# Two graph layers on one core: left and right projections as one product by two levels of Strassen's recursion

## The chip, the cores and the metric

The kernel runs on one core of a Trainium2 chip, in fp32. The metric is the device time of one execution in microseconds, as the median of several runs; lower is better. The engines are named as the profile names them: PE (TensorE, with PEld for its weight loads), DVE (VectorE), ACT (ScalarE), POOL (GpSimd) and SP (SyncE, which only issues DMAs).

## The reference, cut to what matters

The input is 128 graphs of 64 nodes with 768 features, and one 64x64 adjacency for each graph. Layer 0 and layer 1 run one after the other, each with a residual and a layer normalisation:

```python
# layer 0, h = x
u = einsum('bld,bmd->blm', h, h) / sqrt(768); p = softmax(u)
attn = p * adjacency;  attn = attn / (sum(attn, axis=2) + 1e-10)
h_left, h_self, h_right = h @ W_left.T + b_left, h @ W_self.T + b_self, h @ W_right.T + b_right
ctx = attn[j > i] @ h_left + diag(attn) * h_self + attn[j < i] @ h_right
x = layernorm(x + relu(layernorm(ctx) * gamma + beta))
# layer 1: 12 heads of 64
q, k, v = x @ Wq + bq, x @ Wk + bk, x @ Wv + bv
scores = q k^T / 8 + beta * adj, masked where adj is 0
x = layernorm(x + softmax(scores) @ v)
```

Most of the arithmetic is in the six projections by 768x768 matrices: left, self and right in layer 0, q, k and v in layer 1.

## The kernel before

**Tiling.** The 8192 tokens are cut into 16 blocks of 512 tokens (four tiles of 128 tokens, eight graphs). A block needs for each projection a product of 512x768 by 768x768. Every such product is already done by one level of Strassen's algorithm in Winograd's form: tokens, inner dimension and columns are halved, and seven products of halves take the place of eight. `combined` forms the sums of the token side on POOL (S1, S2, S4 and one in place), `prepare` formed the sums of the weight side once at the start and left them in device memory (`pieces` for self, left, right and v; `qk_d` for q and k).

**The schedule of one projection** is the function `seven`. It walks through the seven factors in the order `ORDER` and for each through two halves j, and does three matmuls of 128x128 by 128x384 (q and k: by 128x256) into one PSUM bank. Two tags, X and Y, of two banks each hold the running sums. After each group of three, `first` or `last` evicts the bank: DVE adds the bias or an earlier part and writes SBUF (lines L301, L395, L413, L502); for q and k, ACT does part of it (L533, L539). The weights of a factor come from device memory by a load that SP issues (L296, L527) into the ring `wst` of four slots.

**The order of the work is written out by hand** (`manual_schedule`). In iteration n of the block loop stand, one after the other, the stages left, right and self of block n + 1, then v of block n, then q and k of block n for three groups of heads. In each stage, `hooks` put other work at given places: the scores and weighted sums of the block before (`scores`, `weighted`), the transposes of the adjacency product (`sides`), the context products (`context0`). Work of DVE and ACT in small pieces lies in two queues, `urgent` and `lazy`; after every group of matmuls `step` takes the next pieces off. `settle(key)` empties the queues of all pieces up to those of a key. `squares` and `turned` bring a block back transposed, through device memory (`x1d`), by loads of ACT's queue and transposes of DVE.

**What the change touches.** `side_part` does left or right, with `lr` as its target: four tiles of 128 x 2 x 768, in which the rows of one half of the partitions hold left, the others right, so that one matmul of `context0` (L428) can use both. `finish` is the last normalisation of a block: statistics on DVE (L242, L243), the normalisation on DVE (L629) and the stores of the output by POOL's queue (L630). The stores of a block's layer-0 result by POOL (L452) wait for DVE's L450.

Of the kernel before, what the change touches and what calls it, by code (L numbers as in the profile page):

```python
# [11 lines left out]
F32 = mybir.dt.float32  # L12
# [5 lines left out]
P = 128  # L18
# [5 lines left out]
T = 4  # L24
# [5 lines left out]
HP = H // 2  # L30
NHG = HC
# [11 lines left out]

@with_exitstack
def gnn_two_layers(ctx: ExitStack, tc, x, adj, wl, bl, ws, bs, wr, br, gamma, beta,
# [7 lines left out]
    tp = ctx.enter_context(tc.tile_pool(name="tp", bufs=2))  # L53
    l0 = ctx.enter_context(tc.tile_pool(name="l0", bufs=1))
    l0t = ctx.enter_context(tc.tile_pool(name="l0t", bufs=T))
    tmp = ctx.enter_context(tc.tile_pool(name="tmp", bufs=2))
    wst = ctx.enter_context(tc.tile_pool(name="wst", bufs=4))
# [20 lines left out]
    bias, affine_of = {}, {}  # L78
    bias["q"], bias["k"] = column(bq, "bq"), column(bk, "bk")
# [12 lines left out]
    for half in range(2):  # L92
        for g in range(2):
            sign = 1 if half == g else -1
            nc.gpsimd.affine_select(
                out=side[half * L : (half + 1) * L, g, :], in_=side[half * L : (half + 1) * L, g, :],
                compare_op=ALU.is_gt, fill=0.0, base=0, pattern=[[-sign, L]], channel_multiplier=sign,
            )


    blocks = {}

# [12 lines left out]

    GAP = (gap, "gap")

    def step(act_free=True):
        for queue in (urgent, lazy):
            if not queue:  # L120
                continue
            kind = queue[0][2] if len(queue[0]) > 2 else None
            if kind == "act" and not act_free:
                continue
            queue.popleft()[1]()
            if kind is None:
                return
# [14 lines left out]

    def prepare(nm, quarter_pool, sum_pool, waits=(0, 0, 0)):

        w = weights[nm].rearrange("(p c) e -> p c e", c=KC)
        src = {(0, 0): w[:, 0:HC, 0:HALF], (0, 1): w[:, 0:HC, HALF:D],
               (1, 0): w[:, HC:KC, 0:HALF], (1, 1): w[:, HC:KC, HALF:D]}
        b = {}  # L150
        for q in ((0, 0), (1, 0), (0, 1), (1, 1)):
            b[q] = quarter_pool.tile([P, HC, HALF], F32, tag="w", name=f"b{q[0]}{q[1]}_{nm}")

            with tc.issue_after(streamed["l"][2]) if nm == "k" else ExitStack():
                nc.sync.dma_start(out=b[q], in_=src[q])
        t5, t6, t4 = (sum_pool.tile([P, HC, HALF], F32, tag="w", name=f"t{i}_{nm}") for i in (5, 6, 4))
        in_sbuf = {1: b[0, 0], 2: b[1, 0], 3: b[1, 1], 5: t5, 6: t6, 7: b[0, 1], 4: t4}
        key = ("w", nm)
        if nm in "slrv":
            d = tc.dram_tile([4, P, HC, HALF], F32, name=f"d_{nm}")  # L160
            pieces[nm] = {1: src[0, 0], 2: src[1, 0], 3: src[1, 1], 5: d[0], 6: d[1], 7: d[2], 4: d[3]}

        def store(i):
            if nm in "slrv":
                if i in (5, 6, 7, 4):
                    nc.gpsimd.dma_start(out=pieces[nm][i], in_=in_sbuf[i])
            else:


                queue, first = (nc.sync, streamed["s"][6]) if nm == "q" else (nc.gpsimd, last_sum[1].ins)  # L170
                with tc.issue_after(first):
                    for hg in range(NHG):
                        queue.dma_start(out=qk_d[hg, i - 1, :, "qk".index(nm)],
                                        in_=in_sbuf[i][:, :, hg * P : (hg + 1) * P])

        def formed(i, out, left, right):
            nc.vector.tensor_tensor(out, left, right, ALU.subtract)  # L177
            store(i)

        def idle():  # L180
            pass

        later(key, *[idle] * waits[0], partial(formed, 5, t5, b[0, 1], b[0, 0]),
              *[idle] * waits[1], partial(formed, 6, t6, b[1, 1], t5), partial(formed, 7, b[0, 1], b[1, 1], b[0, 1]),
              *[idle] * waits[2], partial(formed, 4, t4, b[1, 0], t6))
        if nm in "qk":
            later(key, lambda: store(1), lambda: store(2), lambda: store(3))
        return in_sbuf
# [32 lines left out]
    def combined(xT, n=None):  # L221

        a11, a12 = xT[:, 0:HC, 0:HTOK], xT[:, HC:KC, 0:HTOK]
        a21, a22 = xT[:, 0:HC, HTOK:NTOK], xT[:, HC:KC, HTOK:NTOK]
        s1, s2, s4 = (tp.tile([P, HC, HTOK], F32, tag=f"S{i}", name=f"S{i}") for i in (1, 2, 4))
        nc.gpsimd.tensor_tensor(s1, a21, a22, ALU.add)
        nc.gpsimd.tensor_tensor(a21, a11, a21, ALU.subtract)
        nc.gpsimd.tensor_tensor(s2, s1, a11, ALU.subtract)
        last_sum[n] = nc.gpsimd.tensor_tensor(s4, a12, s2, ALU.subtract)
        return {1: a11, 2: a12, 3: s4, 4: a22, 5: s1, 6: s2, 7: a21}  # L230
# [23 lines left out]
    def seven(width, factors, first, last, hooks, taps_by_act=False):  # L254

        X, Y, u = {}, {}, {}  # L260
        for k, i in enumerate(ORDER):
            for j in range(2):
                for f in hooks.get(2 * k + j, ()):
                    f()
                if i == 1:
                    X[j] = ps_st.tile([P, 512], F32, tag="X", name="ps_X")
                if i in (2, 5):
                    Y[j] = ps_st.tile([P, 512], F32, tag="Y", name="ps_Y")
                ps = (X if i in (1, 6, 7, 4) else Y)[j][:, 0:width]
                fs = factors(i, j)  # L270
                for c, (a, b) in enumerate(fs):
                    nc.tensor.matmul(ps, lhsT=a, rhs=b, start=(c == 0 and i in (1, 2, 5)), stop=(c == len(fs) - 1),  # L272
                                     skip_group_check=True)
                if i == 1:
                    u[j, 1] = first(j, 0, ps)
                elif i == 2:
                    last(j, 0, 0, ps, u[j, 1])
                elif i == 6:
                    u[j, 2] = first(j, 1, ps)
                elif i == 7:  # L280
                    u[j, 3] = first(j, 1, ps)
                    last(j, 1, 1, Y[j][:, 0:width], u[j, 3])
                elif i == 4:
                    last(j, 1, 0, ps, None)
                elif i == 3:
                    last(j, 0, 1, ps, u[j, 2])
                step(not taps_by_act or (i, j) not in ((5, 1), (7, 0)))

    def by_tokens(nm, S, last, in_sbuf=None, hooks={}):
# [3 lines left out]
        def factors(i, j):  # L293
            if i not in wt:
                wt[i] = wst.tile([P, HC, HALF], F32, tag="w", name=f"w{nm}")
                streamed.setdefault(nm, []).append(nc.sync.dma_start(out=wt[i], in_=pieces[nm][i]).ins)  # L296
            return [(S[i][:, k, j * P : (j + 1) * P], wt[i][:, k, :]) for k in range(HC)]

        def first(j, b, ps):
            u = tmp.tile([P, HALF], F32, tag=f"u{b}", name="u", bufs=4 if b else 2)  # L300
            nc.vector.tensor_tensor(u, ps, bias[nm][:, b * HALF : (b + 1) * HALF], ALU.add)  # L301
            return u

        seven(HALF, factors, first, lambda j, m, n, ps, part: last(2 * m + j, n, ps, part), hooks)

# [11 lines left out]
    def attention0(n):  # L317
# [18 lines left out]
        blk["S"] = combined(xT, n)  # L336
# [63 lines left out]
    def side_part(n, nm, in_sbuf, hooks={}):  # L400
# [7 lines left out]
        def last(t, h, ps, part):  # L408
            cols = slice(h * HALF, (h + 1) * HALF)
            for g in range(2):  # L410
                rows = slice(g * L, (g + 1) * L)
                half = g if nm == "l" else 1 - g
# [3 lines left out]
        by_tokens(nm, blk["S"], last, in_sbuf, hooks)  # L416

# [99 lines left out]
    def projected(n, hg, hooks={}):  # L517
# [6 lines left out]
        def factors(i, j):  # L524
            if j == 0:
                wt[i] = wst.tile([P, 2, HC, P], F32, tag="w", name="wqk")
                nc.sync.dma_start(out=wt[i], in_=qk_d[hg, i - 1])  # L527
            return [(wt[i][:, j, k, :], S[i][:, k, :]) for k in range(HC)]

        def first(j, b, ps):  # L530
            u = tmp.tile([P, HTOK], F32, tag=f"u{b}", name="uqk", bufs=4 if b else 2)
# [14 lines left out]
    def scores(n, hg, at_once=1, pool=None):  # L546
# [8 lines left out]
        s = l1s_p.tile([P, T, 2, 2, L], F32, tag="s", name="s")  # L555
# [68 lines left out]

    def finish(n, tiles=range(T)):
# [28 lines left out]
    bias["l"] = row(bl, "bl")  # L654
# [3 lines left out]
    bias["r"] = row(br, "br")  # L658
# [28 lines left out]
    blocks[0]["S"] = combined(blocks[0]["xT"])  # L687
    start.close()
# [12 lines left out]
    for n in range(NBLK):  # L701
# [11 lines left out]

        last = n == NBLK - 1
        if p >= 0:
# [4 lines left out]
            at(three, 0 if not last else 6, finish, p)  # L720

        if not last:
            if n > 0:
# [32 lines left out]
                at(own, 11, sums1)  # L756
                if m + 1 < NBLK:
# [8 lines left out]
                side_part(m, "l", None, left)  # L766
                side_part(m, "r", None, right)
# [3 lines left out]
            if m + 1 < NBLK:  # L771
# [5 lines left out]

                def sums0():
                    settle(("t", m + 1))
                    attention0(m + 1)  # L780

                at(qk[0], 4, sums0)
# [3 lines left out]
        else:  # L786
            transposed1(n)
            at(qk[0], 9, lambda: later(("m", n), *mask(n), queue=urgent))
            blocks[n]["S"] = combined(blocks[n]["xT"])
        at(qk[1], 2, scores, n, 0)  # L790
# [45 lines left out]
```

## Time and profile before

| | |
|---|---|
| time, median of 3 runs (lowest, highest) | 2991.72 us (2988.51, 2993.49) |
| the profiled execution, own time | 2993.9 us |
| its span from the first to the last instruction | 2992.2 us |
| one block in the steady state, of that left, right, self, v, q and k | 182.26 us: 33.04, 27.09, 27.09, 33.64, 61.40 |
| busy share of PE, DVE, ACT, POOL | 98%, 72%, 23%, 11% |
| moved by DMA | 541.20 MB, mean 181 GB/s |

A line of the groups names the source line, the engine, the operation, what it writes and reads, its shape and count, then the busy time, the mean of one in ns, and the idle time of its engine before it with what ended it. One fp32 matmul stands as two records in the profile. In a line of the timeline the start and the length come first; instructions of one kind that follow each other are merged, with their count. "A <- B" says that A's wait ended with B.

### The profile page before, as it was taken

Reading aid. Unit: us, or ns where it says so; the run is one execution under the profiler, and the core shown is the slowest. Engines: PE = TensorE matmul, PEld = TensorE weight load, DVE = VectorE, ACT = ScalarE, POOL = GpSimd, SP = SyncE. Lnnn points to the kernel's source line nnn. Section 1 sums busy time; section 2 is a strip of 40 time slices with the busy share of each in tenths; the row PEclk is TensorE's granted clock in tenths of the full one; section 3 lists DMA queues with packets and bytes.
Section 4 is the critical chain, followed back from the end, with each engine's and each line's share of the span. In section 5 each row is a group of like instructions: output and inputs, shape, how many; then the busy total and the mean of one; then the engine's idle time right before and its main releaser. Section 6 shows DMA issues by size and latency. Waiting matters only on the chain.

```text
span 2992.2 us, 45095 instructions
## 1 busy us (share of the span) xinstructions
PE 2927.3 (98%) x17760; PEld 1981.9 (66%) x17760; DVE 2158.1 (72%) x4331; ACT 677.8 (23%) x1360; POOL 339.0 (11%) x297
## 2 busy tenths in 40 slices
PE   8999999999999999999999999999999999999996
PEld 5557667585675857658576675766758566585684
DVE  5857767677776777767777686777767777677657
ACT  0103214031140412304032140321404113040342
POOL 2131020110201101011110201102011020111010
PEclk9999999999999999999999999999999999999998
DMA  8673756747576574765847567475664757557343
GB/s 292 197 264 122 225 157 179 213 134 226 146 200 188 158 214 140 208 176 161 225 130 214 163 178 218 124 235 147 189 198 149 218 143 207 176 159 212 120 122 109
DMA packets 268130, 541.20 MB, mean 181 GB/s; under 512 B 28576, under 2 KB 173472, under 8 KB 267920
## 3 DMA queue, kind: packets, MB, share of 16 engines
q1 hardware_dynamic: 193824, 433.51, 47.3%
q10 hardware_dynamic: 60848, 44.05, 8.1%
q0 software_dynamic: 13248, 60.76, 5.0%
q8 instruction: 141, 2.31, 0.3%
q14 instruction: 69, 0.57, 0.1%
HBM read 473.37 MB, written 64.88 MB: 180 GB/s over the span
## 4 chain that ended last, share of the span: by engine, by line
PE 88%; issue 7%; DVE 3%; DMA 1%; POOL 1%; POOLq 0%; ACTq 0%; SPq 0%; DVEq 0%
PE ps_X L272 46%; PE ps_Y L272 35%; PE ps_ctx L428 3%; PE sc L563 2%; PE u L334 1%; PE ps_y L609 1%; DVE lr L413 1%; DVE eT L585 0%; DMA d_v<-t_v 0%; DMA b_s<-in_L_gnn_W_self_dram 0%; DMA b_k<-in_L_gnn_Wk_dram 0%; DVE o L438 0%; PE ps_a L382 0%; DVE t_s L177 0%; DMA bk<-in_L_gnn_bk_dram 0%
## 5 line engine op out<-in xcount | busy, mean ns | idle before, releaser
L272 PE MATMUL ps_X<-xT,wqk 128*128 128x256 f32 x1728 | 390.9, 380 | 3.4 <-ACT uqk L533 3.4
L533 ACT ACTIVATE uqk<-ps_X,bq 128x256 f32<-128x256 f32 x144 | 68.3, 474 | 1345.6 <-PE ps_X L272 1345.2
L272 PEld LDWEIGHTS ps_X<-xT,wqk 128*128 128x128 f32 x1728 | 329.7, 191 | 52.1 <-ACT uqk L533 3.8
L581 ACT ACTIVATE eT<-s 32x256 f32<-32x256 f32 x768 | 317.7, 414 | 149.8 <-DVE s L590 139.7
L272 PE MATMUL ps_Y<-S,wqk 128*128 128x256 f32 x1152 | 264.3, 379 | 0.0
L413 DVE TENSOR_TENSOR lr<-ps_Y,u 64x384 f32<-64x384 f32 x384 | 213.0, 555 | 66.3 <-PE ps_Y L272 57.1
L272 PEld LDWEIGHTS ps_Y<-S,wqk 128*128 128x128 f32 x1152 | 218.9, 190 | 29.8
L272 PE MATMUL ps_X<-wv,xT 128*128 128x384 f32 x576 | 195.3, 489 | 0.1
L242 DVE BATCH_NORM_STATS2 stats<-o 128x6 f32<-128x384 f32 x384 | 190.2, 537 | 0.4
L272 PE MATMUL ps_X<-wl,hT 128*128 128x384 f32 x540 | 185.4, 489 | 1.5 <-DVE u L301 1.5
L272 PE MATMUL ps_X<-ws,hT 128*128 128x384 f32 x540 | 182.4, 493 | 3.0 <-DVE u L301 3.0
L272 PE MATMUL ps_X<-wr,hT 128*128 128x384 f32 x540 | 179.1, 486 | 0.0
L619 DVE SCALAR_TENSOR_TENSOR o<-ps_y,rz,o 128x64 f32<-128x64 f32 x768 | 165.0, 278 | 6.8
L272 PEld LDWEIGHTS ps_X<-wv,xT 128*128 128x128 f32 x576 | 108.1, 190 | 81.3 <-issue 9.0
L272 PEld LDWEIGHTS ps_X<-ws,hT 128*128 128x128 f32 x540 | 103.7, 193 | 76.6 <-DVE u L301 3.6
L272 PEld LDWEIGHTS ps_X<-wr,hT 128*128 128x128 f32 x540 | 102.5, 190 | 71.3
L301 DVE TENSOR_TENSOR u<-ps_X,bv 128x384 f32<-128x384 f32 x96 | 52.9, 551 | 129.3 <-PE ps_X L272 129.3
L272 PEld LDWEIGHTS ps_X<-wl,hT 128*128 128x128 f32 x540 | 100.3, 190 | 64.0 <-DVE u L301 2.2
L541 DVE TENSOR_TENSOR q<-ps_Y,uqk 128x256 f32<-128x256 f32 x144 | 60.1, 418 | 112.4 <-ACT uqk L533 59.8
L272 PE MATMUL ps_X<-S,wqk 128*128 128x256 f32 x576 | 138.2, 385 | 0.0
L272 PE MATMUL ps_Y<-xT,wqk 128*128 128x256 f32 x576 | 135.6, 385 | 0.0
L272 PE MATMUL ps_Y<-wv,S 128*128 128x384 f32 x384 | 133.2, 490 | 0.0
(183 smaller groups left out, 4489.1 us busy)
## 6 DMA issues: line engine op xcount, KB each, us to landing
wqk<-qk_d SPq DMA_DIRECT2D x336, 384.0 KB, 3.0
wv<-d_v SPq DMA_DIRECT2D x64, 576.0 KB, 4.7
ws<-d_s SPq DMA_DIRECT2D x60, 576.0 KB, 4.5
wl<-d_l SPq DMA_DIRECT2D x60, 576.0 KB, 4.7
wr<-d_r SPq DMA_DIRECT2D x60, 576.0 KB, 4.7
wv<-in_L_gnn_Wv_dram SPq DMA_DIRECT2D x48, 576.0 KB, 4.0
ws<-in_L_gnn_W_self_dram SPq DMA_DIRECT2D x45, 576.0 KB, 3.9
wl<-in_L_gnn_W_left_dram SPq DMA_DIRECT2D x45, 576.0 KB, 4.3
```

The source lines that it names most:

```text
L242: nc.vector.bn_stats(stats[:, h, :], tiles[t][:, h * HALF : (h + 1) * HALF])
L272: nc.tensor.matmul(ps, lhsT=a, rhs=b, start=(c == 0 and i in (1, 2, 5)), stop=(c == len(fs) - 1), skip_group_check=True)
L301: nc.vector.tensor_tensor(u, ps, bias[nm][:, b * HALF : (b + 1) * HALF], ALU.add)
L334: nc.tensor.matmul(u[g * L : (g + 1) * L, t, :], lhsT=xT[:, c, tok], rhs=xT[:, c, tok], start=(c == 0), stop=(c == KC - 1))
L413: nc.vector.tensor_tensor(lr[t][half * L : (half + 1) * L, g, cols], ps[rows], bias[nm][rows, cols] if part is None else part[rows], ALU.add)
L428: nc.tensor.matmul(ps[g * L : (g + 1) * L, 0:HALF], lhsT=blk["aT"][:, t, g * L : (g + 1) * L], rhs=blk["lr"][t][:, g, cols], start=True, s ...
L533: nc.scalar.activation(u, ps, AF.Identity, bias=bias["qk"[j]][:, c : c + 1])
L541: nc.vector.tensor_tensor(dst, ps, part, ALU.add)
L563: nc.tensor.matmul(sc[r][g * L : (g + 1) * L, t, c, :], lhsT=q[rows, c, tok], rhs=k[rows, c, tok], start=True, stop=True)
L581: nc.scalar.activation(e[cols, :, rows], pairs[rows, :, cols], AF.Exp)
L609: nc.tensor.matmul(y[r, h][cols, t, c, :], lhsT=eT[rows, 2 * h + t, c, cols], rhs=v[rows, 2 * h + t, g, hg + c * HC, :], start=True, stop= ...
L619: nc.vector.scalar_tensor_tensor(res[:, r, c, hg, :], ps[:, t, c, 0:HD], rz[:, t, c : c + 1], res[:, r, c, hg, :], ALU.mult, ALU.add)
```

## The change

**Left and right as one product.** From block `DEEP` = 3 on, `both_sides` takes the place of the two calls of `side_part`. Its columns are the left and right columns side by side (2 x 192 in one matmul). On the first level there are seven factors as before; each is done by a second level of the same recursion (`nested`): tokens 256 into 2 x 128, columns 384 into 2 x 192, and of the three inner chunks of 128 two by the recursion and the third in the ordinary way. A second-level product is one matmul (j = 1, 6, 7) or two (j = 2, 5, 4, 3), and is evicted by one instruction into `u_deep` or straight into a quarter of the result. The first-level sums of the results are formed in place in `lr`, partly on POOL. The token side's second-level sums come from `second_level` on POOL. The products of two factors overlap: the order is 6, 5, 7 of one, 1, 2 of the next, 4, 3 of the first.

**Weights.** `deepened` makes the second-level weight sums from `pieces` in iterations 0 and 1 and leaves them in `lr_d`: nine matrices for each of seven factors. All weights of the block loop now come in chunks of 128x384 (192 KB) into a ring of 19 slots, where whole factors of 384 to 576 KB came into four.

**The rest.** Left always lies in the lower partitions of `lr`, right in the upper; for blocks from 3 on, ACT copies swap two of the four parts (`swapped`, in the self stage), and `side` changes with it. `finish_by_act` does the last normalisation with ACT (two passes with sums, one that normalises), except for the block before the last and the last. `step` has a `light` form that runs no DVE piece except tiny ones. S1, S2 and S4 are single buffers, the fourth sum has a function of its own (`combined4`), and the sums of the next block are formed in the third head group and not in the first.

```diff
+ORDER2 = (7, 1, 2, 6, 5, 4, 3)
+MATRICES = (1, 2, 8, 3, 9, 5, 7, 4, 6)
+DEEP = 3
...
-    wst = ctx.enter_context(tc.tile_pool(name="wst", bufs=4))
+    wst = ctx.enter_context(tc.tile_pool(name="wst", bufs=19))
...
-    def step(act_free=True):
+    def step(act_free=True, light=False):
...
+            if light and (queue is lazy or kind is None):
+                return
...
+    def deepened(i):
...
+        def begin():
+            for j, nm in enumerate("lr"):
+                src = pieces[nm][i]
+                for k in range(2):
+                    w[j, k] = wst.tile([P, 2, QUAD], F32, tag="w", name="w_deep")
+                    nc.sync.dma_start(out=w[j, k], in_=src[:, k, :].rearrange("p (h c) -> p h c", h=2))
...
+        def formed(j):
+            b11, b12, b21, b22 = (w[j, k][:, h, :] for k in range(2) for h in range(2))
+            for out, a, b in ((b11, b12, b11), (b12, b22, b12), (b22, b22, b11), (b21, b21, b22)):
+                nc.vector.tensor_tensor(out, a, b, ALU.subtract)
...
+    def second_level(F):
...
+        h0, h1 = slice(0, P), slice(P, 2 * P)
+        q = s2_p.tile([P, 5, P], F32, tag="q", name="q")
+        nc.gpsimd.tensor_tensor(q[:, 0, :], F[:, 0, h1], F[:, 1, h1], ALU.add)
+        nc.gpsimd.tensor_tensor(q[:, 1, :], q[:, 0, :], F[:, 0, h0], ALU.subtract)
+        nc.gpsimd.tensor_tensor(q[:, 3:5, :], F[:, 0::2, h0], F[:, 0::2, h1], ALU.subtract)
+        nc.gpsimd.tensor_tensor(q[:, 2, :], F[:, 1, h0], q[:, 1, :], ALU.subtract)
...
+                wt[i] = [wst.tile([P, HALF], F32, tag="w", name=f"w{nm}") for _ in range(HC)]
+                for k in range(HC):
+                    load = nc.sync.dma_start(out=wt[i][k], in_=pieces[nm][i][:, k, :])
...
+    def nested(width, sums, load, multiply, view, C, bias0, bias1, hooks):
...
+        def taken(i, q, ps, dst, add):
+            if add is None:
+                nc.scalar.copy(dst, view(ps))
+            else:
+                nc.vector.tensor_tensor(dst, view(ps), add, ALU.add)
...
+        def sub(i, j):
...
+            if j == 1:
+                X[i] = ps_st.tile([P, 512], F32, tag="X", name="ps_X")
+            if j in (2, 5):
+                Y[i] = ps_st.tile([P, 512], F32, tag="Y", name="ps_Y")
+            ps = (X if j in (1, 6, 7, 4) else Y)[i][:, 0:width]
+            multiply(F[i], W[i], j, ps)
...
+            step(len(done) > 8, j in (5, 1, 4))
...
+            for j in (6, 5, 7):
+                sub(i, j)
+            if after:
+                sub(after, 1)
+                sub(after, 2)
+            for j in (4, 3):
+                sub(i, j)
...
+    def both_sides(n, hooks):
...
+        def load(i):
+            w = {}
+            for k in (1, 2, 8, 6, 5, 9, 7, 4, 3):
+                w[k] = wst.tile([P, HALF], F32, tag="w", name="wlr")
+                nc.sync.dma_start(out=w[k], in_=lr_d[i - 1, MATRICES.index(k)].rearrange("p s c -> p (s c)"))
+            return w
...
+        def swapped(t):
+            low, high = lr[t][0:L, 1, :], lr[t][L:P, 0, :]
+            swap = l1s_p.tile([P, T * 4 * L], F32, tag="s", name="swap")
+            nc.scalar.copy(swap[0:L, 0:D], high)
+            nc.scalar.copy(high, low)
+            nc.scalar.copy(low, swap[0:L, 0:D])
...
-            at(three, 0 if not last else 6, finish, p)
+            at(three, 0 if not last else 6, finish if last else finish_by_act, p)
...
+                if m < DEEP:
+                    side_part(m, "l", None, left)
+                    side_part(m, "r", None, right)
...
+                else:
+                    for t, f in enumerate(both_sides(m, {**left, **{2 * len(ORDER) + k: f for k, f in right.items()}})):
+                        at(own, 1 + t, f)
```

## The prediction, made before the changed kernel was run

> **What bounds the kernel now.** I read the page's busy times and chain first, then a table of busy time by stage for one block in the middle, then the timeline of single banks.
>
> ```profile
> PE 2927.3 (98%) x17760; PEld 1981.9 (66%) x17760; DVE 2158.1 (72%) x4331; ACT 677.8 (23%) x1360; POOL 339.0 (11%) x297
> ...
> PE 88%; issue 7%; DVE 3%; DMA 1%; POOL 1%; POOLq 0%; ACTq 0%; SPq 0%; DVEq 0%
> ```
>
> TensorE (PE) is the bound, 98% busy and 88% of the chain. The stages of one block (left, right, self, values, queries and keys) say it more sharply; the columns are length, then busy us of PE, weight loads, VectorE (DVE), ScalarE (ACT), GpSimd (POOL), clock, DMA share, GB/s:
>
> ```profile
> 1585.17:1618.21 33.04, 31.70 (x282) 19.33 (x281) 24.38 (x53) 12.39 (x28) 1.63 (x3) 1.00 0.84 222
> 1618.21:1645.30 27.09, 27.09 (x86) 15.96 (x85) 22.86 (x59) 0.20 (x1) 1.08 (x2) 1.00 0.70 220
> 1645.30:1672.39 27.09, 27.09 (x86) 15.96 (x85) 19.25 (x27) 0.00 (x0) 8.10 (x6) 1.00 0.74 217
> ```
>
> Right and self take the same 27.09 us although DVE, POOL and DMA differ: there PE waits for nobody. A stage holds 42 products of 128x384, two records each (84), so one record is 27.09/84 = 0.3225 us, and the chain has the same: 24 records in 7.74 us.
>
> ```profile
> 1633.85 7.74 PE ps_X L272 x24
> ```
>
> Left has 5.94 us more: score and weighted products of the block before, and transposes, hooked in between. So fewer records pay in full, as long as PE still waits for nobody. Two timeline excerpts say how long a wait for a bank (PSUM) would be.
>
> ```profile
> 1585.17 2.10 PE L272 MATMUL ps_X<-wl,hT 128*128 128x384 f32 x6
> ...
> 1587.31 0.56 DVE L301 TENSOR_TENSOR u<-ps_X,bl 128x384 f32<-128x384 f32 x1 [0.92 <-PE ps_X L272]
> ```
>
> The sixth record's slot ends at 1585.17 + 6 x 0.3225 = 1587.105; DVE starts 0.20 us later and takes 0.56 (0.555 in the groups of L413).
>
> ```profile
> 128.14 0.54 DVE L301 TENSOR_TENSOR u<-ps_X,bs 128x384 f32<-128x384 f32 x1
> ...
> 128.75 3.52 PEld L272 LDWEIGHTS ps_X<-ws,S 128*128 128x128 f32 x12 [0.55 <-issue]
> 128.78 4.11 PE L272 MATMUL ps_X<-ws,S 128*128 128x384 f32 x12
> ...
> 132.73 4.03 PE L272 MATMUL ps_Y<-ws,S 128*128 128x384 f32 x12
> ```
>
> Here PE had waited for an eviction: released 0.07 us after its end (128.68), and twelve records later it stands at 132.73, not 128.78 + 3.87 = 132.65: a restart costs about 0.1 us more, the weight load that is no longer hidden. From the end of a product to the restart of a product that needs its bank: 0.20 + 0.555 + 0.06 + 0.10 = **0.915 us**, with DVE free.
>
> ```profile
> 1599.71 0.55 DVE L301 TENSOR_TENSOR u<-ps_X,bl 128x384 f32<-128x384 f32 x1
> 1600.17 0.17 DVE L615 RECIPROCAL rz<-ps_y 128x4 f32<-128x4 f32 x1
> 1600.38 0.86 DVE L619 SCALAR_TENSOR_TENSOR o<-ps_y,rz,o 128x64 f32<-128x64 f32 x4
> 1601.15 0.17 DVE L615 RECIPROCAL rz<-ps_y 128x4 f32<-128x4 f32 x1
> ```
>
> Back to back, DVE starts the next instruction 0.46 us after an eviction (I use 0.49), and one queued piece of "added" work lasts 1601.15 - 1600.17 = 0.98 us.
>
> **What the Trainium skill says.** "VectorE: DVE Perf Modes", its section on the TRN2 errata, prices a PSUM read at 120 + 384 cycles of 0.96 GHz = 525 ns; the trace has 555, which I use. "SBUF — State Buffer", Who interferes with whom: an instruction of DVE with one SBUF input doesn't contend with GpSimd, one with two does. The trace agrees: beside a POOL sum an eviction keeps 0.56 us, while the SBUF-only sum of L485 takes 1.92 us for 256 elements. The new POOL work therefore doesn't lengthen evictions. "DMA: Bandwidth & Descriptors", Specifications, gives 435 GB/s as the fabric's ceiling; this trace moves 386 GB/s from 9 to 30 us, at a share of 1.06, and I take that as full.
>
> **The change part by part.** *Fewer products.* From block 3 on, left and right become 7 x 7 sub-products of 128x(2x192), 11 matmuls for each of 7 instead of 12: 77 for 84. Saved: 7 matmuls = 14 records = 4.515 us a block, 13 blocks: **-58.7 us**, all on the path.
>
> *New waits for banks.* Before, between two uses of a bank lay the other half's three matmuls, 1.935 us, against 0.915 needed. Now a product with j = 1, 6, 7 is one matmul (0.645 us), the others two (1.29); the order for one factor i is 6, 5, 7, 1', 2', 4, 3 (' = next factor), 7.095 us. Each tag has two banks, and 2 and 5 each open a Y bank: 5 of the next factor takes the bank of 3, and only 6 lies between. Wait A: 0.915 - 0.645 = 0.27 us, six times a block, 1.62. Wait B: in the last factor 4 follows 7 directly, 0.92. Wait C: the queued pieces. The two "weighted" hooks each put four pieces of 0.98 us behind evictions. Where one follows 3's eviction (0.20 to 0.69), 6's eviction runs from 1.67 to 2.22 and 7 can start at 2.38, where it was due at 0.915 + 1.29 = 2.205: 0.18, about twice a block, 0.36. In all 2.90 us a block, x 13 = **+37.7 us**. Bounds: 1.5 us a block if the restart is hidden and C vanishes; 5.8 if evictions of the new form take 0.70 instead of 0.555. DVE's demand in a factor with four pieces is 7 x 0.49 + 4 x 0.98 = 7.35 us for 7.4: just enough.
>
> *DVE and ACT.* Evictions of left and right: 44 before (12 of L301, 32 of L413), 49 now, 4 of them ACT copies: DVE's sum is unchanged. The normalisation that ends a block leaves DVE (8 x 0.537 + 4 x 0.208 + 4 x 0.68 = 7.9 us) for 12 ACT passes of 768. ACT's rows of 256 (0.475) and 1536 (1.475 us) make 0.875 for 768: 10.5 us, and 12 swap copies of 64x768 as much, where ACT has 41.6 of 182 us now. It relieves a DVE that delays nobody: counted at nothing. DVE's tiny steps wait for the sums (3.5 us) 4.5 us after they could start. If ACT is late, the evictions behind those steps are, then PE; a us or two a block is the upper bound. The swaps stand in the self stage, 27 us, before the context that needs them.
>
> *POOL.* Per block 28 instructions of second-level sums (640 elements a factor) and 12 sums of 384. At L226's 1.81/768 = 2.4 ns an element, an estimate, that is 10.6 + 10.9 us in a stage where POOL is busy 2.7 us. A factor's sums can start when 3 of the factor before last ends and are first needed by its 6, 7 us later. Behind the x1d issues, which wait for DVE's normalisation (L450), stand the sums of the third factor, due well after. First-level sums move to the last head group, since their buffers are single: 7.7 us of products cover two of 1.81. Counted at nothing; if late, each us is on PE.
>
> *DMA and SP.* Left and right load 63 x 192 KB = 12.4 MB instead of 8.3; with what else moved (222 and 220 GB/s over 60.1 us, 13.3 MB) 17.4 MB in some 58 us, 300 GB/s of 386. Nineteen slots let a load start 8 to 9 us before its use; landing took 4.7 us for 576 KB. All weights of a block are 147 issues on SP for 49, at 0.33 us (the tile view of d_v): 48 of 180 us. The stores of the output and x1d stay on POOL. Hidden; at worst 2 or 3 us a block, where the transposing loads of sq (207 GB/s at a share of 1.10) coincide.
>
> *Start.* Making the deep weights: 56 subtractions of 192 elements on DVE (about 0.35 us each, by L301's size), 28 loads and 56 POOL issues, beside the products of blocks 0 to 2. I take +3 us; -4 to +8, since chunks can also arrive earlier.
>
> Sum: -58.7 + 37.7 + 3 = -18.0. The profiled execution took 2993.9 us (span 2992.2), 2.2 above the median 2991.7: 2975.9 there, **2974** as a median.
>
> **Rivals.** *All saved* (0.10): the waits are hidden, -58.7 + 3, 2936. For it: PE never waits in the stages shown. Against: only one matmul lies between the uses of the Y bank. *DVE as the bound* (0.15, the slower side): the form 2x192 or its SBUF operand costs more than 0.555. At 0.70, spaced 0.66, A is 0.41, B 1.06, and factors with four pieces need 8.5 us of DVE for 7.1: 5.8 us of waits a block, +16 us, with the start +19, 3011. It decides from about 0.64 us an eviction, where the waits reach 4.5. Against it: 64x384 and 128x384 forms both take 0.555. *Weights late* (0.10): 2.5 us more a block, +32.5 on my sum, 3006; for it, DMA shares of 0.84 already, and packets of 1.5 KB. *No gain* (0.08): the recursion saves 14 records but the start and small waits by ACT and POOL eat the rest, 2990.
>
> **How the numbers follow.** My case has 0.57, with 2962 to 2988 as its own range. About 0.2% (6 us) is what a measurement of this kernel tells from no change. My case's upper end adds to "same", its rest and the first rival to "faster": 0.68 faster, 0.15 same, 0.17 slower. The range leaves out most of the first rival and the worst of two others: 2950 to 3002.
>
> **What would show it.** In the profile after, left and right together should take 60.1 - 1.6 = 58.5 us; PE should show idle of 0.2 to 0.3 us behind DVE's L416 at each fifth product, 0.9 at the end; evictions of L416 0.55; POOL some 22 us more a block; s, v and q/k stages unchanged at 27.09, 33.64, 61.40. I'm wrong if that stage is under 56 or over 60 us, if L416 takes over 0.64, or if PE waits there for DMA or POOL.

## The result, and the profile after

The changed kernel takes **2977.3 us** (median of 5 runs, 2975.3 to 2979.7) where the kernel before took 2991.7 beside it (5 runs, 2988.5 to 2993.7): 0.9954 times as long, 95% interval 0.9939 to 0.9968. That is 14.4 us less, where 18 had been forecast. The profiled execution has a span of 2978.0 us (before 2992.2).

The page's busy times and chain, changed kernel:

```profile
PE 2881.8 (97%) x17578; PEld 1940.8 (65%) x17578; DVE 2062.7 (69%) x4219; ACT 994.4 (33%) x1848; POOL 713.0 (24%) x881
...
PE 79%; DVE 6%; issue 6%; ACT 5%; DMA 3%; POOL 1%; SPq 0%; ACTq 0%; POOLq 0%; DVEq 0%
```

PE works 45.5 us less but is busy for a smaller share, and the chain, 88% PE before, now passes through DVE and ACT for 11%: part of the saving has turned into waits. The table by stage (same columns as before) says where. The first row is left and right of a middle block, now one stage, the second is self:

```profile
685.87:743.87 58.00, 55.31 (x352) 32.33 (x350) 42.65 (x102) 26.17 (x53) 30.41 (x46) 1.00 0.97 291
743.87:770.96 27.09, 27.09 (x86) 15.96 (x84) 17.88 (x24) 9.96 (x12) 5.56 (x3) 1.00 0.81 238
```

Left and right were 33.04 + 27.09 = 60.13 us and are 58.00: 2.1 us a block, of the 4.515 that seven matmuls fewer make. Self, values and q/k kept 27.09, 33.64 and 61.40 to 0.01 us. So the sum of the profiled execution is: 13 blocks x -2.12 = -27.6; the start, up to the first such stage, +14.15 (505.75 us from the span's start instead of 491.60); a few late weights in three blocks +4.6, which the runs below hardly showed again; and from the last such stage to the end -5.2. Together -14.1, against spans 14.2 apart. Of the -5.2, 4.1 lie between the issue of the last store and the end of the span, 8.03 us before and 3.94 after. The packets of that store take 2.3 us in both; what differs is the time from the last packet to the end, 5.8 us and 1.7. The profile doesn't say why, so this part is no work that the change saved. The start also varies: in the runs below that leave its preparations as they are, the first such stage begins between 504.6 and 511.3 us. The two big terms are what the experiments are about.

**Inside a steady stage.** I took the distance of each matmul record from the last and noted what it has above 0.3225 us. Four waits and the hooks make up the 2.39 us that were paid back: product 6 of the first factor (number 7) 1.66; product 7 of two factors, for the bank of 6, 0.45 each; the last product 4 0.92; the score hook 0.42 more than before, the second weighted hook 1.52 less, since it no longer waits for transposes. The timeline around the first of these:

```profile
687.12 3.39 ACT L796 ACTIVATE eT<-s 32x256 f32<-32x256 f32 x8
...
690.31 0.46 POOL L314 TENSOR_TENSOR q<-hT 128x128 f32<-128x128 f32 x1
690.53 0.48 ACT L414 COPY u_deep<-ps_X 128x384 f32<-128x384 f32 x1
690.54 1.30 DVE L800 STREAM_TRANSPOSE eT<-eT 128x512 f32<-128x512 f32 x2 [2.85 <-ACT eT L796]
...
691.11 0.88 PE L613 MATMUL ps_X<-wlr,q 128*128 128x384 f32 x2 [1.43 <-POOL q L314]
```

The bracket blames POOL, as does the list of PE's waits (1.4 us here, 17.0 in all). But two instructions end just ahead of the restart: POOL's sum at 690.77 and ACT's copy at 691.01, which is the eviction of the bank that this product needs. 691.11 is 0.10 after the copy, close to the 0.07 that the prediction read between an eviction's end and the restart. And the copy is late because eight exponentials stand before it in ACT's queue. They were no later before the change. There the stage began at 1585.17, and this line stands in its timeline:

```profile
1586.41 3.40 ACT L581 ACTIVATE eT<-s 32x256 f32<-32x256 f32 x8
```

The exponentials end 4.64 us after the stage's start, as they do now (690.51 against 685.87), but no eviction of left or right was ACT's. Two suspects, then; the first experiment parts them.

The eviction itself behaves as forecast:

```profile
L416 DVE TENSOR_TENSOR lr<-ps_Y,u_deep 128x384 f32<-128x384 f32 x273 | 151.5, 555 | 75.1 <-PE ps_Y L613 66.9
```

**At the start.** The left stage of the second pass (for block 2) takes 48.75 us instead of 33.03:

```profile
334.79 2.50 DVE L666 TENSOR_SCALAR o<-o,mv,rstd 128x768 f32<-128x768 f32 x4
335.76 2.35 POOL L668 DMA_DIRECT2D x1d<-o  x4 [22.17 <-DVE o L666]
...
342.04 2.92 ACTq L275 DMA_DIRECT2D sq<-x1d  x3
...
346.29 3.40 ACT L796 ACTIVATE eT<-s 32x256 f32<-32x256 f32 x8
...
349.72 1.30 DVE L800 STREAM_TRANSPOSE eT<-eT 128x512 f32<-128x512 f32 x2 [6.83 <-ACT eT L796]
...
350.58 2.01 PE L824 MATMUL ps_y<-v,eT 64*64 64x65 f32 x64 [13.76 <-DVE eT L800]
```

Read from below: PE waits 13.8 us for transposed exponentials, DVE for ACT, and ACT issues its second half only after it has got the reloads `sq<-x1d` off, whose source was stored late, since all four pieces of the normalisation (L666) came from 334.8 on. Ahead of them DVE runs subtractions of `deepened`, 4.62 us from 303.3 and 1.54 us from 333.1. In the kernel before, the four pieces (L450) began at 305.4, 308.6, 309.9 and 323.3, and all the exponentials went out ahead of the reloads:

```profile
322.81 6.81 ACT L581 ACTIVATE eT<-s 32x256 f32<-32x256 f32 x16 [8.84 <-DVE s L590]
323.29 0.67 DVE L450 TENSOR_SCALAR o<-o,mv,rstd 128x768 f32<-128x768 f32 x1
...
329.34 2.41 ACTq L205 DMA_DIRECT2D sq<-x1d  x4
```

### The profile page after: what moved, and what is told of

It reads as the page before. It is cut to its first block, busy times and chain, and to the rows that moved or that the text cites. A ratio compares the mean times of both kernels' runs of the same rounds, so it can differ in the third digit from the quotient of the medians.

```text
span 2978.0 us, 49826 instructions
## 1 busy us (share of the span) xinstructions
PE 2881.8 (97%) x17578; PEld 1940.8 (65%) x17578; DVE 2062.7 (69%) x4219; ACT 994.4 (33%) x1848; POOL 713.0 (24%) x881
## 4 chain that ended last, share of the span: by engine, by line
PE 79%; DVE 6%; issue 6%; ACT 5%; DMA 3%; POOL 1%; SPq 0%; ACTq 0%; POOLq 0%; DVEq 0%
PE ps_X L362 32%; PE ps_Y L362 24%; PE ps_Y L613 9%; PE ps_X L613 8%; PE ps_ctx L644 3%; ACT eT L796 3%; PE u L504 1%; PE ps_y L824 1%; PE sc L778 1%; DMA wlr<-lr_d 1%; ACT L796 1%; DVE lr L416 1%; DVE mx L804 1%; DVE s L782 1%; DVE s L805 0%
## 5 line engine op out<-in xcount | busy, mean ns | idle before, releaser
L296 POOL TENSOR_TENSOR S<-hT 128x768 f32<-128x768 f32 x16 | 28.9, 1808 | 1157.3 <-PE ps_Y L362 1120.3
L613 PE MATMUL ps_Y<-wlr,q 128*128 128x384 f32 x546 | 208.6, 491 | 0.0
L416 DVE TENSOR_TENSOR lr<-ps_Y,u_deep 128x384 f32<-128x384 f32 x273 | 151.5, 555 | 75.1 <-PE ps_Y L613 66.9
L613 PE MATMUL ps_X<-wlr,q 128*128 128x384 f32 x364 | 150.1, 494 | 23.9 <-POOL q L314 17.0
L416 DVE TENSOR_TENSOR u_deep<-ps_X,lr 128x384 f32<-128x384 f32 x195 | 107.8, 553 | 60.4 <-PE ps_X L613 54.7
L613 PEld LDWEIGHTS ps_Y<-wlr,q 128*128 128x128 f32 x546 | 101.6, 190 | 67.2
L296 POOL TENSOR_TENSOR S<-xT 128x768 f32<-128x768 f32 x16 | 28.9, 1806 | 452.3 <-DVE xT L284 323.8
```

What stands on the lines that cost most here:

```text
L416: nc.vector.tensor_tensor(dst, view(ps), add, ALU.add)
L613: nc.tensor.matmul(ps, lhsT=a, rhs=b, start=(k == 0 and j in (1, 2, 5)), stop=(k == len(fs) - 1), skip_group_check=True)
```

## The experiments

In this part "the stage" is that of left and right of a steady block, and a ratio is to runs of the kernel before on the same chip.

**Who holds product 6 of the first factor?**

```diff
-            taken(i, q, ps, U[i, k], part(i, q))
+            if (i, k) == (7, 1):
+                nc.vector.tensor_copy(U[i, k], view(ps))
+            else:
+                taken(i, q, ps, U[i, k], part(i, q))
```

> One edit to the changed kernel: the very first eviction of a left-and-right stage (factor 7, product 1) is a DVE copy and no longer an ACT copy. Theory: product 6 of factor 7 waits 1.66 us a block for this eviction, because ACT still runs eight exponentials of the stage before (3.4 us) when the product is ready; on DVE it is done in time, 13 x 1.66 = 21.6 us go, 2955 to 2958 us. Rival: the wait is for the second-level sums of POOL, as the list of waits names it (L314); then nothing changes, 2975 to 2980 us.

Measured: 2971.65 us, ratio 0.9928 (0.9913 to 0.9943); the stage 57.30, 0.69 less and not 1.66. Its timeline:

```profile
691.87 0.81 PE L616 MATMUL ps_X<-wlr,q 128*128 128x384 f32 x2
...
692.65 0.45 POOL L314 TENSOR_TENSOR q<-hT 128x128 f32<-128x128 f32 x1
...
692.88 1.30 DVE L803 STREAM_TRANSPOSE eT<-eT 128x512 f32<-128x512 f32 x2 [2.39 <-ACT eT L799]
...
695.29 0.54 DVE L416 TENSOR_TENSOR lr<-ps_Y,u_deep 128x384 f32<-128x384 f32 x1
...
695.88 1.56 PE L616 MATMUL ps_Y<-wlr,hT 128*128 128x384 f32 x4 [0.62 <-DVE lr L416]
```

Product 6 now runs at 691.87, without a wait and before POOL's sum has begun: POOL was never the cause. But DVE stands 2.39 us for the same exponentials, to transpose them, and the next evictions stand behind it: PE stops 0.89 us in another place, and one of the 0.45 grows by 0.08. 1.66 - 0.97 = 0.69. The cause isn't which engine copies; it is that the exponentials end 4.6 us after the stage begins.

**Is the predicted wait A absent because of how banks are handed out?** The prediction had product 5 wait for the bank of the factor's own predecessor, 0.27 six times. Here each Y bank gets its own fixed use:

```diff
-                Y[i] = ps_st.tile([P, 512], F32, tag="Y", name="ps_Y")
+                Y[i] = ps_st.tile([P, 512], F32, tag="Y0" if j == 2 else "Y1", name="ps_Y", bufs=1)
```

The one-level function `seven` gets the same (tags Y0 and Y1 for its two halves).

> One edit to the changed kernel: the two Y banks have tags of their own, so that product 5 of a factor always takes the bank in which product 3 of the factor before was summed. Theory: this is the wait of 0.27 us, six times a block, that the prediction counted and the profile does not show, because the pool hands out the bank that was released first, that of product 2; forced, it costs 6 x 0.27 x 13 = 21 us, 2995 to 3002 us. Rival: the wait was counted wrongly and evictions hand a bank back sooner than that; then 2975 to 2980 us.

Measured: 2993.2, ratio 1.0003 (0.9994 to 1.0012); the stage 59.28, 1.28 more. Six products 5 now wait, 0.17 to 0.26 plus 0.10 of restart each, 1.82 in all where wait A was priced at 1.62; the two waits C get 0.27 shorter each in return. The stages of `seven` kept 27.09, 33.64 and 61.40, so the 1.28 is that of the two-level stage. So A was priced right and isn't there: with two buffers of one tag, product 5 gets the one released earlier.

**Where do the waits C come from?**

```diff
-            step(len(done) > 8, j in (5, 1, 4))
+            step(len(done) > 8, j in (5, 1, 4, 3))
```

> Edit: after product 3 of a factor only a tiny queued step may be issued to VectorE, not one of the long ones, so that the eviction of the next factor's 6 isn't behind a piece of 0.98 us. Theory (wait C): the two places where 7 of a factor waits for the bank of 6, 0.373 us and 0.075 of restart each, 0.90 us a block, come from the queued piece ahead of that eviction. Then left and right together should fall by 0.9, from 58.00 to 57.1 us a block, and 13 blocks by 11.7: about 2966. Rival: VectorE's queue has no room, the piece that isn't placed there goes ahead of another eviction and the same wait appears elsewhere; then the stage stays at 58.0 and the time at 2977, within 2 us.

Measured: 2979.27, ratio 0.9962 (0.9947 to 0.9977); the stage 57.84 to 57.97. Both waits C are gone, 0.90, so the queued piece ahead of 6's eviction was their cause; but the second weighted hook takes 2.06 us instead of 1.31, because its transposes, in the same queue, come later. The rival was right on the time.

**What is the rest worth?** First without the second level: `DEEP = 99` and no deepening; the swaps, which belong to the second level, go with it, and everything else is as changed. Then with the second level, but the normalisation by DVE as before.

```diff
-            at(three, 0 if not last else 6, finish if last else finish_by_act, p)
+            at(three, 0 if not last else 6, finish, p)
```

> The changed kernel without the recursion: left and right as two products of one level in all blocks, no deep weights made; what stays is chunks of weights in 19 slots, ACT's last normalisation, single buffers of the sums and the fixed sides. Theory: PE waits for none of these before or after, so they are worth nothing: 2986 to 2993 us, like the kernel before. Rival: relief of DVE or finer weights bring part of the gain by themselves: below 2984 us; or single buffers and chunks cost: over 2996 us.

> Edit: the last normalisation of every block goes back to VectorE (8 x 0.54 + 4 x 0.21 + 4 x 0.68 us, 7.9 us a block, in the stage of left and right), all else as in the changed kernel. Theory: moving it to ScalarE is worth nothing, as the prediction counted; the stage stays at 58.0 (57.7 to 58.3) us and the time at 2977, 2973 to 2981. Rival 1: VectorE has no room in that stage, where each eviction stands behind the queued steps, so steps come later and products wait for banks: 0.5 to 1 us more a block, 2984 to 2990. Rival 2: ScalarE's passes make the copies of evictions late; without them the stage gets shorter by up to 1 us a block, 2964 to 2970.

Measured: the rest alone 2993.43, ratio 1.0001 (0.9992 to 1.0010): nothing, and its stages have the lengths of the kernel before (33.03, 27.09, 27.09, 33.64, 61.40). The second level with DVE's normalisation 2994.03, ratio 1.0005 (0.9996 to 1.0014): nothing either, the stage 59.25 to 59.60, with DVE busy 47.97 us of it instead of 42.65, and new waits of 0.69, 0.47 and 0.09 for evictions (the last is 0.45 in the stages of 59.60). Together they gain 14. Rival 1 was right, and larger than it said: relieving DVE is worth nothing as long as each bank has 1.9 us of other products behind it, and 1.3 us a block once it has 1.3 or 0.6. The worth is measured; that the cover of the banks makes it is read from where the new waits stand, and no run varies the cover alone.

**The exponentials.** The first attempt hooked the score products four sub-products later (place 3 for 1) and the weighted ones at 8 for 5.

> Edit: from block 3 on, the score products of the last head group are hooked four sub-products later in the stage of left and right (after the first factor's first five), and the weighted products of the middle head group six later. The hook of the scores makes ScalarE take all pending exponentials and VectorE the transposes that wait for them, ahead of the evictions that follow in their queues. Theory: the 1.66 us by which product 6 of the first factor waits is these exponentials (3.39 us) ahead of the first copy of ScalarE, and giving that copy to VectorE gained 0.69 only because VectorE stands in wait for the same exponentials. With the hook later both evictions come first: 1.66 a block and part of the scores' own 0.42 go, the stage falls to 56.0 to 56.5 us, the time to 2952 to 2958. Rival: the exponentials only stand ahead of other copies or make the weighted products late; the stage falls by 0.7 or less, 2968 to 2977.

Measured: 3094.38, ratio 1.0341 (1.0324 to 1.0358); the stage 66.5 to 68.1. Both theory and rival fell. The exponentials end 4.6 us after the stage's start, as in the changed kernel: they stand in ACT's queue before the hook, put there by the steps of the q/k stage. The 1.6 us of scores had merely filled part of the wait: product 6 now waits 3.3 us. The later scores then bring the last transposes later, and an eviction behind them holds PE for another 2.6. And there is a price on top, in the table by stretch:

```profile
700.44:703.76 3.32, 3.32 (x5) 1.81 (x6) 1.70 (x3) 0.48 (x1) 1.33 (x3) 0.50 0.52 182
704.10:708.00 3.90, 3.90 (x73) 2.47 (x72) 2.51 (x5) 0.48 (x1) 0.56 (x1) 1.00 0.38 102
```

The third figure from the end is the clock. After the stop of 3.1 us PE runs at 0.50 for 3.3 us, and each record takes 0.64 us instead of 0.32.

The second attempt asks why the exponentials are issued so late. In the changed kernel VectorE's subtraction is done at 674.9, but the first four go out at 682.7: the four "added" pieces of the first head group's weighted products had been put ahead of them in the queue.

```diff
-            at(qk[2], 5, weighted, n, 0)
+            at(qk[2], 11, weighted, n, 0)
```

> Edit: in the last head group of queries and keys the weighted products of the first head group are hooked at place 11 instead of 5, so that their four 'added' pieces of 0.98 us no longer stand in the urgent queue ahead of the exponentials of the middle head group; nothing else. Theory: product 6 of the first factor waits 1.66 us because ScalarE's sixteen exponentials (1.70 us for four), ready at the end of VectorE's subtraction, 674.88 in the profile after, are issued only from 681.38 on, behind those pieces, and the last eight end 4.66 us after the stage of left and right begins, with the first copy of an eviction behind them. Issued earlier, they end before the stage begins: the 1.66 goes and the scores' wait of 0.42 may, the stage takes 56.0 to 56.4 us instead of 58.0, the time is 2951 to 2957. Rival 1: the exponentials now delay the evictions of queries and keys by up to 1.7 us each, the q/k stages grow from 61.40 to 62 or more and eat half of it or all: 2962 to 2978. Rival 2: the displaced 'added' pieces fall into the stage of left and right and make other evictions late, as with the normalisation on VectorE: 57 to 58 us, 2965 to 2977.

Measured: 2957.73, ratio 0.9886 (0.9871 to 0.9900). ACT in its timeline, with one line of PE:

```profile
673.88 3.40 ACT L796 ACTIVATE eT<-s 32x256 f32<-32x256 f32 x8
677.30 0.47 ACT L748 ACTIVATE uqk<-ps_X,bq 128x256 f32<-128x256 f32 x1
...
677.83 1.56 PE L362 MATMUL ps_X<-xT,wqk 128*128 128x256 f32 x6 [0.59 <-ACT uqk L748]
...
680.37 1.69 ACT L796 ACTIVATE eT<-s 32x256 f32<-32x256 f32 x4
...
685.25 0.48 ACT L414 COPY u_deep<-ps_X 128x384 f32<-128x384 f32 x1 [2.68 <-PE ps_X L613]
```

The last exponential ends at 682.06, 2.3 us before the stage begins, and the copy at 685.25 waits for PE, not PE for it. The stage takes 55.91: the 1.66 and the 0.42 are gone, exactly. Rival 1 was right as well: eight exponentials hold one eviction of a q/k product, and that stage goes from 61.40 to 62.27.

**The start.** The deep weights are made by pieces that go to the front of the urgent queue. First, one of them moves from the left to the self stage of the second pass:

```diff
-                                                    (0, qk[2], 6), (1, left, 2), (1, right, 4))):
+                                                    (0, qk[2], 6), (1, own, 2), (1, right, 4))):
```

> One edit to the changed kernel: the deep weights of factor 4 are made in the self stage of iteration 1 and no longer in its left stage. Theory: in that left stage the pieces that form them stand ahead of the second half of the exponentials in the urgent queue, so that these fall behind the loads of sq on ACT's queue, which wait for the stores of x1d; the weighted products then wait 13.8 us once. With the pieces gone from there, this wait goes: 2962 to 2966 us. Rival: the loads of sq themselves are late, or the extra DMA traffic of the deep weights is what delays; then the wait stays or moves, 2973 to 2980 us.

Measured: 2966.59, ratio 0.9913 (0.9898 to 0.9927); the left stage 39.1 instead of 48.75. In that run the four normalisations, 2.5 us, stand just ahead of the transposes, PE stops 2.8 and 1.2 us for these, and its clock falls to 0.50 there; the stops and the slower clock together are enough for the 6.1 us that remain. Next, the last three factors in the right, self and values stages:

> Edit: the deep weights of the last three factors are made during the right, self and values stages of the second block's pass (before: one in the last head group of the first block's pass, one in left, one in right); nothing else. Theory: VectorE's eight subtractions of 0.55 us each, which stand in an urgent queue ahead of the normalisation of the first block and of its score steps, cost the 6.1 us that remained in that left stage (39.13 against 33.03) when one of them was moved. Then the left stage takes 33 to 34 us, and the time falls by 14 to 15.7 us against the changed kernel: 2961 to 2963. Rival: another cause (the stores of x1d, weights from the dram tiles behind other loads) holds that stage; it stays at 38 to 40 us, 2965 to 2968.

Measured: 2982.04, ratio 0.9965 (0.9953 to 0.9977). The left stage stays at 38.1, and the first stage at two levels takes 70.85 instead of 58.0. The timeline of that stage:

```profile
532.26 13.05 ACTq L275 DMA_DIRECT2D sq<-x1d  x4
545.40 0.84 ACT L865 ACTIVATE unused<-o 128x768 f32<-128x768 f32 x1 [25.96 <-DMA wlr<-lr_d]
...
549.27 0.17 DVE L851 TENSOR_SCALAR f<-f 128x4 f32<-128x4 f32 x1 [9.05 <-ACT unused L865]
549.35 0.55 DVE L416 TENSOR_TENSOR u_deep<-ps_X,lr 128x384 f32<-128x384 f32 x1
...
549.96 1.65 PE L613 MATMUL ps_X<-wlr,S 128*128 128x384 f32 x2 [6.58 <-DVE u_deep L416]
```

The left stage of the second pass holds no subtractions any more, so they aren't what keeps it at 38.1. In the stage at two levels it is the same chain one block later: block 2's normalisation (blocks counted from 0) comes later, its stores go out between 500 and 528, the last 29.9 us after the stage begins instead of 13.8, ACT stands 13 us in the issue of the reloads, the new ACT normalisation starts late, a DVE step waits 9 us for its sums, an eviction waits behind that step, and PE for the eviction. It is the case "ACT late" of the prediction, and costs 12.9 us where it occurs. The subtractions themselves end at 435.9; that they push the normalisation back through the queues is argued, not shown. The 25.96 in ACT's bracket names a weight load, but ACT's sequencer was taken by the reloads up to 545.31. Last, the places as they were, but the pieces at the end of the queue (`urgent.extend`):

> Edit: the subtractions that make the deep weights go to the end of the urgent queue instead of its front; their places, loads and stores stay. Theory: the 14 us that the change costs at the start come from these pieces standing ahead of the first block's normalisation, whose four pieces (2.5 us) then stand ahead of the transposes that the weighted products wait for, and whose stores make the reloads late. Then the left stage of the second block's pass takes 33 to 35 us instead of 48.75, nothing comes back in the first stage of left and right at two levels (58.0), and the time is 2962 to 2965. Rival: behind the queue the deep weights are late; the products of the first stage of left and right at two levels wait for them, or the slots of weights stay taken longer and the loads of blocks 0 and 1 come late: that stage takes 62 us or more or earlier stages grow, and the time is 2970 to 2985.

Measured: 2980.08, ratio 0.9963 (0.9949 to 0.9977); the left stage 49.97. The theory fell: here it makes no difference whether the pieces stand at the front or at the end of the queue. Now the score steps are late instead, and the exponentials with them. The queues give out one long piece per product, and whatever stands in them, the extra pieces use up as many products; I argue this from the traces, no run isolates it.

**Together.**

> Edit: the two edits that gained, together: exponentials earlier (weighted products of the first head group at place 11) and one deepening in the self stage of the second block's pass. Theory: they act in different stages and add up: 2957.7 - 10.7 = 2947, 2944 to 2950. Rival: the start is held by something else as soon as the exponentials move there too; 2953 to 2958.

> Edit: as the run before, and in the stages of queries and keys no piece for ScalarE is issued after the first of the two products number 5, so that four of the sixteen exponentials at a time, not eight, stand ahead of the eviction of the products number 7. Theory: the 0.86 us by which the q/k stages grew (62.27 for 61.40) is that one eviction, held 0.6 us behind eight exponentials of 3.40 us, and the restart; it goes, 13 times 0.86 is 11 us: 2936, 2933 to 2940; the last four exponentials then stand behind the first copy of ScalarE in the stage of left and right, which stays at 55.9 to 56.3 us. Rival: the last exponentials, 1.7 us later, are late again for VectorE's transposes, and the stage of left and right takes 56.7 us or more: 2946 or above.

```diff
-                step(not taps_by_act or (i, j) not in ((5, 1), (7, 0)))
+                step(not taps_by_act or (i, j) not in ((5, 0), (5, 1), (7, 0)))
```

Measured: both 2948.44, ratio 0.9856 (0.9839 to 0.9872), the gains add up. With the slot **2940.56**, ratio **0.9831** (0.9816 to 0.9845): q/k back at 61.40, the stage still 55.91. That is 50 us below the kernel before and 37 below the changed one, and what remains of the waits in a stage is C twice, 0.90, and B, 0.92.

## Why the prediction was right, point by point

The time was within 4 us because errors cancelled, and that is luck: the forecast of the blocks was 6.6 us too high and that of the finish 5, while the start was 11 us too low and the 4.6 of late weights weren't in the sum. Of the 5 at the finish, 4.1 are no work of the kernel's at all. The direction and the main term were understood; the waits were the right kind of cost in partly the wrong places.

- *Fewer products, -58.7*: right; the records keep 0.3225 us, and the other stages don't change.
- *Wait A, 1.62 a block*: the step that failed is "5 of the next factor takes the bank of 3". The price was right (1.28 net, by the run with fixed banks), but the banks are handed out by release.
- *Wait B, 0.92*: measured 0.815 + 0.104 = 0.92.
- *Wait C, 0.36 a block*: right place, cause (the run without a piece after 3) and end: 7 was to start 2.38 us after the end of 3, and started at 2.31 and lost 0.075 more at its next record. But it was held to be due at 0.915 + 1.29 = 2.205, with wait A in it; without A it is due at 0.645 + 1.29 = 1.935, and the wait is 0.45 instead of 0.18. The run that brings A back shortens C by that 0.27. So one wrong step sits in two terms: A and C together 1.98 forecast, 0.90 found.
- *ACT, counted at nothing, "a us or two if late"*: the step that failed. Its copies had no cover, since ACT works off eight exponentials just then: 1.66 a block, and 0.42 in the score hook. The prediction looked at the copies as DVE's relief and never asked what stands ahead of them in ACT's queue, though the trace before had the exponentials end 4.64 us after the stage begins.
- *The normalisation on ACT, counted at nothing*: wrong for the changed kernel. Keeping it on DVE costs 1.3 us a block. The argument, that DVE delays nobody, came from a trace in which the waits for banks had 1.9 us of cover.
- *The hooks*: not in the sum; 1.1 us a block less than before.
- *Sum of a block*: 2.90 forecast to be paid, 2.39 paid; 58.5 against 58.00.
- *POOL, 21.5 us a block, hidden*: 26.8 (second-level sums 2.1 a factor, sums of 384 1.00 each, not 0.9), and hidden, though a bracket says otherwise. *DMA, 300 GB/s, hidden*: 291 at a share of 0.97, hidden but for 4.6 us in the one profile.
- *Start, +3, at most +8*: the worst term, 14.15. The subtractions were counted as work (20 us of DVE beside products), not as places in a queue whose other pieces have stores, reloads and exponentials behind them. The moved deepening shows 10.7 of it; the other 3.5 are not taken apart.
- *Finish*: nothing was counted, and -5.2 was found. 4.1 of it is the shorter time from the issue of the last store to the end of the span: 8.03 us before and 8.68 in the run without the second level, 3.9 to 4.1 in every run with it. The cause stays open.

"All saved" failed on B, C and the exponentials; "DVE as the bound" on 555 ns for an eviction; "weights late" needs 2.5 us a block, and there were 4.6 in all. "No gain" named the right mechanism, small waits by ACT and the start, at too large a size. Of the signs named, the stage's length (58.00 for 58.5), the 0.9 at its end, the 0.55 of L416 and the unchanged stages came true; POOL took more, 26.8 for 22, and the idle at each fifth product did not come. PE's waits do name POOL, 17.0 us, which was to show the prediction wrong, but POOL wasn't the cause.

## What to carry to other kernels

Where products get shorter, price every eviction by the queue that it stands in: list what is ahead of it on its engine at that moment, on the engine that is idle on average as well, and ask what that work waits for. An engine's relief that is worth nothing in the kernel before can be worth the whole gain after. And preparations that run once still take places in a queue; look at what they push behind, above all stores that something reloads.

## What the runs showed of the hardware

A long stop of PE can cost more than its length. The Trainium skill ("TensorE: Matmul & The Clock Gate", Part 1) says that the array's clock halves after about 3.4 us of idleness and comes back after as much work. The traces agree that it halves: 0.50 for 3.3 to 5.8 us after stops of 3.1, 6.6 and 13.8 us. So the stop of 3.1 us cost another 1.8. They don't agree on how much idleness it takes, and here the measurement decides. In the run with the later scores, PE stops for 2.46 us at the same place of each stage. In one block 0.50 follows, and in the next it doesn't:

```profile
720.92:724.33 3.41, 0.95 (x4) 0.36 (x3) 3.30 (x11) 0.00 (x1) 0.97 (x2) 1.00 1.08 250
724.34:727.75 3.41, 3.41 (x9) 2.08 (x9) 2.77 (x12) 0.00 (x0) 0.00 (x0) 0.50 1.10 244
...
908.66:912.07 3.41, 2.80 (x9) 1.33 (x7) 1.32 (x3) 2.00 (x5) 2.00 (x4) 1.00 0.93 234
912.07:915.48 3.41, 1.56 (x8) 1.15 (x9) 3.27 (x14) 0.00 (x0) 0.00 (x0) 1.00 1.14 207
915.48:918.90 3.42, 3.42 (x42) 1.95 (x40) 3.25 (x11) 0.00 (x0) 0.00 (x0) 1.00 1.06 298
```

In all fourteen traces the clock changes only at steps of 3.41 us (to within 6 ns), and the rows are such steps. The first stop lies in one step, which has 0.95 us of PE work. The second is split, and the two steps have 2.80 and 1.56. Over the 11,755 steps of these traces at 1.00, up to 70 us before the end, every step with more than 1.95 us without a matmul record was followed by 0.50, and none with less than 1.77 was; between the two, both occur.

A bracket names the releaser that the records allow, not always the true one: POOL was named for 1.4 us of a wait that ended with ACT's copy, 0.24 us later.
